# Last-layer products of five sequences among the scans instead of three, and spiking neurons of four on GpSimd instead of three

## The chip, the cores and the metric

The kernel runs on one core of a Trainium2 chip. [...] The metric is device time in microseconds (us) of one launch, stated as the median of several runs.

## What is computed

Eight layers run over 8 sequences of 512 tokens with 128 channels, all in float32. The change touches the end: the state-space mixer of the last but one half layer, its gated feed-forward, and the last layer, a feed-forward whose output goes through a spiking neuron. Cut from the reference, for one sequence `x` (512 x 128):

```python
# mixer: normalise, causal convolution, per-channel step sizes dt, then a scan over time
h[t] = exp(dt[t] * A) * h[t-1] + dt[t] * u[t] * Bmat[t]        # 128 channels x 48 states
y[t] = sum_over_states(h[t] * Cmat[t]);  x = x + y @ out_proj_w.T + out_proj_b
# gated feed-forward
u = rmsnorm(x);  x = x + (silu(u @ gate_w.T) * (u @ up_w.T)) @ down_w.T
# last layer
n = layernorm(x);  c = square(relu(n @ W_fc.T)) @ W_proj.T
mem = 0
for _ in range(5):                      # spiking neuron with a constant input c
    mem = 0.9 * mem + c - reset;  spike = mem > 1;  count += spike
x = x + count / 5
```

The number of spikes in five steps only rises with `c`, so the kernel counts how many of five constants (`SPIKES`) lie below `c`.

## The kernel before

The work that matters is in `l2_attn_l3_attn`. Its last block runs the scans: for each sequence b of 8, four quarters q of the channels, three groups g of 16 states, two halves j. One step of the inner loop makes two pairs of small products into a PSUM tile `bx` (L1879, PE), the decay `a` by an exponential (L1885, ACT), and the scan itself over 128 x 1024 elements (L1890, DVE), 192 scans in all. `give` sums over the states one group later (L1690, PE, tile Z) and multiplies by the gate at a quarter's end (L1698, DVE, tile zx). The inputs of a quarter come from DRAM two quarters ahead (`fetch`, `fetch_dt`, SP's queue), and `products` multiplies the loaded gx by xk on POOL (L1335 in the profile, 128 x 1024 elements) one quarter ahead in the program.

All other work is cut into Python generators, whose steps are placed between the scans. `step(gens)` advances every generator of a list by one yield; `in_turn` chains generators. The list `side` is stepped once behind each group, three times per quarter. It holds:

- `prepare(b)`: normalisation, convolution and step sizes of a later sequence (b + 2 during b). It uses the tiles xn (tag x1, 8 buffers), u, up, xh, dt, du (2 buffers each, up one), and lp and two (one buffer each), the last two for a polynomial on POOL. It is finished for sequence 7 during b = 5.
- `project(b)`: after the last quarter of b: sums over states (L1709), the output projection (L1719, L1720), sums of squares on ACT (L1917), the normalised u (L1732), transposes and copy to hT (L262, L267), two gate products with Silu (L1744, L1746), two up products (L1751, L1752), the down products (L1757), the sum into X[b] with its statistics (L1761, L248, L249). It ends by adding b to `given`.
- `layer_3b(b, tail)`: the last layer up to its output c. It waits (in the program's order) for b in `given`; then normalises (L1122), transposes and copies (L262, L265), makes four products with W_fc (L1795), a Relu and a Square each on ACT (L1803, L1805), then 16 products with W_proj (L1818, each recorded as two), and copies c to a tile y (L1827). With tail False, each of the four products is a step with a PSUM tile of its own and the 16 products are two steps, 8 steps in all; with tail True the four products are two steps and the 16 one, 5 steps, and PSUM comes from the tiles bx and Z of the ended scans.
- `slow_neurons(b)`: the count on POOL: two operations per constant, the sum into X[b] and a store from POOL's own queue (L1849 to L1857). It takes its two work tiles from a gx buffer (tag gx, three buffers, which the scans' loads use).

`neurons(b)` does the count on DVE in five operations and the sum in one (L1835 to L1839), and stores from SP's queue.

PSUM has eight banks: the tag mm (two tiles of one bank) serves prepare, project and layer_3b with tail False; bx takes four banks in two tiles, Z two.

The order is written out by hand by the place of each step: layer_3b of sequences 0 to 2 enters `side` at quarter (5, 3), slow_neurons of 0 to 2 at (7, 2). Behind the last scan, layer_3b of 3 to 7 is stepped with tail True beside what is left in `side`, and neurons(3) to neurons(7) follow as their inputs appear. On each engine the framework may put an instruction ahead of earlier ones in the program that wait for something, as long as tiles and data allow. Layer_3b's normalisation is on POOL for sequences 0 to 4 and on DVE for 5 to 7.

## Time and profile before

| | us |
|---|---|
| median of 3 runs (lowest to highest) | 1713.37 (1712.08 to 1717.24) |
| the profiled execution's own time | 1725.08 |
| its span, first to last instruction | 1723.3 |
| first scan starts | 1129.8 |
| quarter (5, 3) starts its scans | 1495.1 |
| last scan ends | 1654.0 |
| PE's last product ends | 1715.4 |
| DVE's last instruction ends | 1719.8 |
| PE busy over the span | 1470.0 |
| DVE busy over the span | 1206.9 |
| ACT, POOL busy over the span | 796.6, 677.8 |

All times inside an execution are counted from its first instruction. A row of the timeline has the start, the duration of the stretch, the engine, the line, the operation, what it writes and reads, how many instructions were merged and, in brackets, how long the engine had been idle before and what it waited for. A row of a table by windows has a stretch, its length, then the busy time of each engine with the number of its instructions, the granted TensorE clock (1.00 is full), the share of the transfer engines and their GB/s; filtered to one line of the program it has only the engines of that line. PEld are weight loads, which overlap PE's products.

### The profile page before, as it was taken

How to read it: one execution, taken by the hardware profiler on the slowest of the kernel's cores; microseconds unless marked ns; L12 is line 12 of the kernel's file. 1: busy time of each engine (PE TensorE's matmuls, PEld its weight loads, DVE VectorE, ACT ScalarE, POOL GpSimd, SP SyncE). 2: the span in 40 equal slices, each digit the busy share in tenths (PEclk: the TensorE clock that was granted, in tenths of full speed). 3: DMA queues.
4: the chain of work that ended last, by engine and by line, in shares of the span. 5: the costliest groups of instructions: out<-in, count | busy, mean ns of one | idle time of the engine just before them, and what ended most of it. 6: DMA issues, size and time to landing. Idle time of an engine off the chain costs nothing.

```text
span 1723.3 us, 22463 instructions
## 1 busy us (share of the span) xinstructions
PE 1470.0 (85%) x8060; PEld 651.2 (38%) x8061; DVE 1206.9 (70%) x2374; ACT 796.6 (46%) x1158; POOL 677.8 (39%) x728
## 2 busy tenths in 40 slices
PE   5978898899888868988999896977888888888887
PEld 2322333334344435644555453422222222233335
DVE  7688666655654444357775764589899999988765
ACT  3655655555454423353223230055555565565634
POOL 4754344443321140211213318135645645712750
PEclk8999899999899889988999898999899999999988
DMA  7991000000000022304544653634444444443201
GB/s 270 384 342 34 1 1 13 7 13 13 13 19 19 13 99 78 95 10 109 124 116 118 134 126 95 151 80 129 124 127 128 133 129 125 131 117 95 61 13 31
DMA packets 94224, 164.69 MB, mean 96 GB/s; under 512 B 10848, under 2 KB 36960, under 8 KB 90016
## 3 DMA queue, kind: packets, MB, share of 16 engines
q1 hardware_dynamic: 89392, 151.97, 31.4%
q0 software_dynamic: 3568, 9.18, 1.7%
q10 hardware_dynamic: 1152, 2.10, 0.4%
q8 instruction: 64, 1.05, 0.3%
q14 instruction: 48, 0.39, 0.1%
HBM read 110.27 MB, written 52.95 MB: 95 GB/s over the span
## 4 chain that ended last, share of the span: by engine, by line
PE 43%; DVE 28%; issue 10%; POOL 7%; ACT 5%; DMA 5%; SPq 1%; DVEq 0%; POOLq 0%; ACTq 0%
DVE h L1890 11%; PE key L1644 5%; PE acc L1622 5%; PE bx L1879 3%; DMA gx<-du_d 2%; PE mm L262 2%; PE sT L568 2%; DVE mf L547 2%; PE o L591 2%; PE sc L536 1%; PE gu L369 1%; PE gu L1055 1%; DMA gate<-gates 1%; DVE zx L1698 1%; PE Z L1690 1%
## 5 line engine op out<-in xcount | busy, mean ns | idle before, releaser
L1890 DVE TENSOR_TENSOR_SCAN h<-a,bx 128x1024 f32<-128x1024 f32 x192 | 426.9, 2269 | 29.2 <-PE bx L1879 27.7
L1885 ACT ACTIVATE a<-dr,nA 128x1022 f32<-128x1022 f32 x192 | 219.4, 1146 | 221.2 <-DVE h L1890 221.0
L1879 PE MATMUL bx<-gx,wb 64*128 64x512 f32 x768 | 220.2, 666 | 61.3 <-DVE h L1890 59.2
L1335 POOL TENSOR_TENSOR gx<-gx,xk 128x1024 f32<-128x1024 f32 x32 | 75.4, 2357 | 226.0 <-DMA gx<-du_d 194.3
L1644 PE MATMUL key<-xT,L_ffn_keys 128*128 128x512 f32 x256 | 136.4, 615 | 22.9 <-DVE act L1648 22.9
L1879 PEld LDWEIGHTS bx<-gx,wb 64*128 64x128 f32 x768 | 64.8, 195 | 195.1 <-DVE h L1890 149.8
L1622 PE MATMUL acc<-act,L_ffn_values 128*128 128x512 f32 x256 | 132.7, 602 | 0.0
L1648 DVE SCALAR_TENSOR_TENSOR act<-key,gate 128x512 f32<-128x512 f32 x128 | 86.5, 685 | 47.8 <-PE key L1644 34.6
L1690 PE MATMUL Z<-h,wc 64*32 64x512 f32 x1536 | 110.3, 628 | 0.1
L547 DVE TENSOR_REDUCE mf<-sm 128x8 f32<-128x1024 f32 x64 | 76.1, 1211 | 42.5 <-POOL sm L543 42.4
L577 POOL TENSOR_SCALAR_AFFINE_SELECT eT<-eT 128x1024 f32<-128x1024 f32 x64 | 68.9, 1099 | 78.7 <-ACT eT L575 78.7
L543 POOL TENSOR_SCALAR_AFFINE_SELECT sm<-sm 128x1024 f32<-128x1024 f32 x64 | 69.4, 1098 | 71.2 <-ACT sm L542 70.9
L1433 POOL DMA_INDIRECT back<-f_out,back_at x32 | 30.8, 964 | 155.7 <-DVE bn L248 139.3
L542 ACT COPY sm<-sc 128x1024 f32<-128x1024 f32 x64 | 62.5, 1014 | 54.7 <-PE sc L536 40.6
L1410 ACT COPY oT<-acc 128x512 f32<-128x512 f32 x8 | 4.7, 587 | 159.2 <-PE acc L1622 159.2
L575 ACT ACTIVATE eT<-sT 128x1024 f32<-128x1024 f32 x64 | 62.0, 1021 | 28.0 <-PE sT L568 27.9
L1644 PEld LDWEIGHTS key<-xT,L_ffn_keys 128*128 128x128 f32 x256 | 47.1, 195 | 73.2 <-issue 36.2
L1622 PEld LDWEIGHTS acc<-act,L_ffn_values 128*128 128x128 f32 x256 | 49.1, 193 | 60.0 <-issue 60.0
L536 PE MATMUL sc<-kb,qT 32*128 32x512 f32 x256 | 58.9, 724 | 10.0 <-ACT sm L542 4.1
L248 DVE BATCH_NORM_STATS2 bn<-x 128x6 f32<-128x128 f32 x224 | 56.1, 272 | 4.8 <-DMA x<-in_L_attn_hidden_states 4.0
L1116 POOL TENSOR_TENSOR rstd<-rstd,minus_half 128x4 f32<-128x4 f32 x27 | 28.0, 1040 | 80.0 <-DVE rstd L1115 79.8
L568 PE MATMUL sT<-qT,kb 32*128 32x512 f32 x256 | 55.2, 655 | 4.5 <-ACT sm L542 2.9
(482 smaller groups left out, 3006.4 us busy)
## 6 DMA issues: line engine op xcount, KB each, us to landing
f_in<-zeros SPq DMA_DIRECT2D x10, 3584.0 KB
gate<-gates SPq DMA_DIRECT2D x128, 256.0 KB
dr<-dt_d SPq DMA_DIRECT2D x32, 1024.0 KB
gx<-du_d SPq DMA_DIRECT2D x128, 128.0 KB
xk<-xh_d SPq DMA_DIRECT2D x32, 256.0 KB
wide<-in_L_ffn_experts SPq DMA_DIRECT2D x1, 3072.0 KB
xg<-f_in SPq DMA_DIRECT2D x48, 64.0 KB
f_out<-ys SPq DMA_DIRECT2D x12, 256.0 KB
```

The lines of the kernel that those rows point to most:

```text
L536: nc.tensor.matmul(halves[q // 2][:, 4 * (q % 2) : 4 * (q % 2) + 4, :], qT[quad(q), cols(c)], kb[quad(q)], start=True, stop=True,)
L543: nc.gpsimd.affine_select(out=sm, in_=sm, compare_op=ALU.is_ge, fill=-1e30, base=0, pattern=[[0, 8], [-1, P]], channel_multiplier=1,)
L547: nc.vector.tensor_reduce(mf[:, c, 2 * i : 2 * i + 2], sm.rearrange("p (q r) k -> p q r k", q=2), AX.X, ALU.max, negate=True,)
L568: nc.tensor.matmul(halves[q // 2][:, q % 2, :], lhs[quad(q), r, :], rhs[quad(q)], start=(k == 0), stop=(k == 1),)
L1335: nc.gpsimd.tensor_tensor(gx, gx, xk.unsqueeze(1).to_broadcast([P, 2, S]), ALU.mult)
L1622: nc.tensor.matmul(acc, f2_v[:, j, :], act, start=(j == 0), stop=(j == J - 1))
L1644: nc.tensor.matmul(key, f2_k[:, 2 * j : 2 * j + 2, :], xT, start=True, stop=True)
L1648: nc.vector.scalar_tensor_tensor(act, key, 0.0, gate[:, j % 2, :], ALU.max, ALU.mult)
L1690: nc.tensor.matmul(zs[q][32 * j : 32 * j + 32, i, :], wcf[half, g, :], hs[j // 2][half, j % 2, :], start=(g == 0), stop=(g == G - 1),)
L1879: nc.tensor.matmul(bx[:, k, :], wbf[half, g, :], gx[half, j, :], start=True, stop=True,)
L1885: nc.scalar.activation(a[:, :, 1:], dr[:, 2 * j : 2 * j + 2, 1:], AF.Exp, scale=nA[:, q, g : g + 1],)
L1890: nc.vector.tensor_tensor_scan(h.rearrange("p r t -> p (r t)"), a.rearrange("p r t -> p (r t)"), bx.rearrange("p r t -> p (r t)"), 0.0, AL ...
```

## The change

Layer_3b of sequences 0 to 4, not 0 to 2, is made with tail False. Its generators leave `side` for a list of their own, `between`, which enters at the same quarter (5, 3) and is stepped inside the loop over j: behind the first half of every group and behind both halves of the middle one, four times per quarter instead of three. What is left of it behind the last scan runs ahead of layer_3b of 5 to 7. slow_neurons counts for sequences 0 to 3, enters `side` already at (5, 3), and takes its work tiles from the tags lp and two of prepare instead of gx. neurons begins at sequence 4. The engine of the normalisation is now chosen by `tail`.

```diff
-                    normal(b, mv4, r, xn, engine=nc.gpsimd if b < NB - 3 else nc.vector)
+                    normal(b, mv4, r, xn, engine=nc.vector if tail else nc.gpsimd)
...
-                    cnt = work.tile([P, 2, S], F32, tag="gx", name="cnt", bufs=3)
-                    n, hit = cnt[:, 0], cnt[:, 1]
+                    n = work.tile([P, S], F32, tag="lp", name="lp", bufs=1)
+                    hit = work.tile([P, S], F32, tag="two", name="two", bufs=1)
...
-                side = []
+                side, between = [], []
+                TAIL = NB - 3
...
                         if (b, q) == (NB - 3, Q - 1):
-                            side.append(in_turn([layer_3b(k, False) for k in range(3)]))
-                        if (b, q) == (NB - 1, Q - 2):
-                            side.append(in_turn([slow_neurons(k) for k in range(3)]))
+                            between.append(in_turn([layer_3b(k, False) for k in range(TAIL)]))
+                            side.append(in_turn([slow_neurons(k) for k in range(TAIL - 1)]))
...
                                 hs.append(h)
+                                if j == 0 or g == 1:
+                                    step(between)
...
-                side.append(in_turn([layer_3b(b, True) for b in range(3, NB)]))
-                done = 3
+                side.append(in_turn([*between, *(layer_3b(b, True) for b in range(TAIL, NB))]))
+                done = TAIL - 1
```

## The prediction

> **What bounds the kernel now.** I read the page first (TensorE, PE, is busy for 85% of the span, VectorE, DVE, for 70%), then cut the last 600 us into stretches at the starts of the scans (L1890). Sequence 4 lasts from 1382.5 to 1445.8, sequence 6 from 1511.0 to 1582.7, sequence 7 from there to 1654.0, the end of the last scan. The quarter (5, 3), where the last layer's generators enter, begins at 1495.1.

> ```profile
> core 0: us, PE busy (x) PEld busy (x) DVE busy (x) ACT busy (x) POOL busy (x), PEclk, DMA share, GB/s
> ...
> 1382.50:1445.80 63.30, 54.97 (x356) 17.66 (x356) 61.23 (x43) 36.42 (x44) 36.08 (x32) 0.95 0.48 130
> ...
> 1511.00:1582.70 71.70, 63.30 (x408) 24.08 (x410) 61.47 (x43) 43.91 (x57) 16.91 (x12) 0.98 0.39 103
> 1582.70:1654.00 71.30, 61.87 (x404) 22.81 (x400) 61.35 (x41) 34.66 (x46) 51.89 (x40) 0.93 0.23 61
> 1495.10:1654.00 158.90, 137.45 (x884) 50.30 (x868) 137.48 (x94) 84.77 (x108) 78.89 (x62) 0.94 0.33 87
> ...
> 1654.00:1716.00 62.00, 55.56 (x280) 36.51 (x280) 29.64 (x59) 33.80 (x63) 7.63 (x6) 0.92 0.08 22
> ```

> Read the length of each stretch against PE's and DVE's busy time. Sequence 4 is DVE's: 61.2 of 63.3 us. Sequences 6 and 7 hold the same DVE work and take 8 us more: they carry 24 steps of layer_3b for sequences 0 to 2, and PE's work has risen from 55 to 62 or 63 us. Over the nine quarters from 1495.1 the two engines are level (137.45 and 137.48), with 21.4 us in which each is idle. Behind the last scan PE alone sets the pace: 55.6 of 62 us. So there are two prices: what layer_3b's products take from the tail, and what they cost among the scans. The next view, the same two stretches for the two product lines alone (L1795, then L1818), gives both; its first figure behind the length is PE.

> ```profile
> 1495.10:1654.00 158.90, 13.50 (x24) 3.57 (x24) 0.94 0.33 87
> 1654.00:1716.00 62.00, 20.77 (x40) 6.41 (x40) 0.92 0.08 22
> ```
> ```profile
> 1495.10:1654.00 158.90, 12.31 (x96) 11.17 (x96) 0.94 0.33 87
> 1654.00:1716.00 62.00, 23.71 (x160) 22.71 (x160) 0.92 0.08 22
> ```

> Three sequences among the scans: (13.50 + 12.31) / 3 = 8.6 us, and 0.66 for the four transposes (the row at 1539.7), 9.3 us of PE each. Five in the tail: (20.77 + 23.71) / 5 + 0.66 = 9.6 us each.

> **How many steps move.** Before, layer_3b steps once per group, 3 per quarter; 9 quarters make 27 steps, and 3 sequences need 8 each. After, step(between) is called 4 times per quarter (for j = 0 of each group, and j = 1 of the middle one): 36 steps, that is four sequences (32) and four steps of sequence 4: normal, transposes, k = 0 and k = 1. Its other four steps open the tail, ahead of 5, 6 and 7. So 12 steps are added among the scans.

> **Tail.** PE loses sequence 3 (9.6 us) and of sequence 4 the transposes and two of four L1795 products (0.66 + 4.15 / 2 = 2.7): 12.3 us. The copies of y (L1827) in the tail are PE's beat: 1675.1, 1688.4, 1698.0, 1706.3, and PE's end at 1715.4; a sequence is worth 8 to 13 us of it. The chain under it, project(7) to given(7), ends at about 1685 (stats behind L1761 at 1683.0) and then normal, transposes and products of sequence 7, some 12 us at the durations of the rows (four normals 1.1, transposes and copy 1.3, four products with their ACT and DVE work 5, 32 products of L1818 4.7): 1697 even with project(7) as slow as now, against 1715.4 - 12.3 = 1703. So PE still ends last and 12 us is my value. The lower bound is 7: project(7) waits for ACT (the Sqrt and Silu tables, 1.28 us each) with less other work to fill PE, and the rest of sequence 4 now takes the same two mm tiles as project(7), where sequence 3 took bx and Z tiles. The upper is 15, if the half clock behind such waits (granted 0.65 from 1671 to 1674 and 0.60 from 1710 to 1713) goes. neurons(3), 3.9 us of DVE (0.43 + 4 x 0.69 + 0.69), also leaves the tail, at no gain: DVE is busy there for 30 of 62 us.

> **Scans.** PE gains 9.3 + 0.66 + 13.50 / 6 = 12.2 us, to 149.6, and becomes the busier engine. How much of it lengthens the 158.9 us depends on the idle 21.4. 14.7 us of that are bx products waiting for a scan (15 waits), which is free room; 6.4 us are three stalls in which PE waits for ACT. Bounds: if all idle time stays, +12.2; if quarters become as tight as the one from 1511.0 to 1526.7 (PE 15.52 of 15.7 us) and 1582.7 to 1597.6 (14.54 of 14.9), some 0.3 to 1.0 us idle each, 149.6 + 9 = 158.6, no change. Another price: 158.9 less nine quarters of sequence 4's 63.3 / 4 is 16.5 us for 24 steps, 0.69 each, 8.3 for 12. I take **+5**: a little below the middle of 0 and 12.2, because waits for scans are two thirds of the idle time and a busier PE has no such waits.

> **GpSimd (POOL).** A sequence of slow_neurons takes 17.3 us (first is_gt at 1627.67, store issued until 1644.94). Before, three run back to back from 1610.3 to 1662.3. After, four, each behind its own y, some 31 us apart (8 steps at 4 per quarter of 15.5 us), so POOL goes from 78.9 us to 78.9 + 17.3 + 7.6 (what now lies behind 1654) = 104 of about 164. What queues behind them is products (L1335, 2.36 us per quarter), project's two steps (1.04 each) and the normals (3.1). POOL waits 68.6 us for the gx loads there, and products for the last quarter ran at 1605.9 for scans from 1639.4: 20 us and more of slack against 17.3. Cost nothing; without that cover, one slow step (2.8 us) per quarter. The 13 scans from 1612 on, with POOL busy all through, take 2255 to 2287 ns like those before (2253 to 2289), so DVE is not slowed. The tiles lp and two were last used by prepare(7) (du at 1496.4), and slow_neurons fills them in order on one engine: no wait for a buffer. The normals of 3 and 4 already run on POOL among the scans (1554.5, 1595.6); the edit of `engine` chooses the same engines as before. ACT gets 6.1 us for sequence 3 (two copies 0.59, four pairs of 0.58 + 0.63) and 3.1 for 4, on 84.8 of 158.9: not a bound in sum, but its order matters below. The stores move from SP to POOL's queue for one sequence, 0.84 us.

> **Sum**: -12 + 5 = **-7 us**, against the profiled execution's own 1725.08 (span 1723.3 and 1.8 around it): 1718.1. That execution is 11.7 us above the median of the runs, 1713.37; the same 7 us off the median give 1706.4.

> **Rivals.**
> *Slower: stalls for the two mm tiles.* The place is the third quarter of a sequence, 25.0 us in sequence 6 and 26.8 in 7 where others take 15. Timeline:

> ```profile
> 1617.14 1.15 ACT L1885 ACTIVATE a<-dr,nA 128x1022 f32<-128x1022 f32 x1 [1.03 <-DVE h L1890]
> 1618.20 0.58 ACT L1803 ACTIVATE du<-mm 128x512 f32<-128x512 f32 x1
> ...
> 1618.83 2.08 PE L1744 MATMUL mm<-hT,L_attn_gate_w 128*128 128x512 f32 x2 [2.53 <-ACT du L1803]
> ...
> 1620.83 3.78 PE L1879 MATMUL bx<-gx,wb 64*128 64x512 f32 x8
> ...
> 1623.03 2.29 DVE L1890 TENSOR_TENSOR_SCAN h<-a,bx 128x1024 f32<-128x1024 f32 x1 [4.80 <-PE bx L1879]
> ```

> project's second gate product needs an mm tile that layer_3b's product filled; ACT empties it only after an exponential that waits for a scan; PE stands for 2.53 us with the next bx products behind, restarts at a granted clock of 0.50 (next row), and DVE loses 4.80 us.

> ```profile
> 1618.80:1621.00 2.20, 2.17 (x4) 0.67 (x5) 0.00 (x0) 2.16 (x3) 2.03 (x3) 0.50 0.00 0
> ```

> Twelve more steps through two tiles can make more of these. 12 / 4.80 = 2.5 further stalls eat the tail's gain; with four the sum is -12 + 19.2 = +7.2, 1720.6. For it: in each of the two sequences the stall came where both generators met. Against: the new calls stand at j = 0, with an exponential and a scan between them and project's step. [...]

> *No change*: PE's 12.2 us come back in full among the scans, -12 + 12.2: 1713.4. For it: PE would be the busiest engine there. Or the tail gives only 7: 1711.

> *Larger gain*: steps apart from project's remove half of the 10 us by which each third quarter is too long: 2 x 5 = 10 less in the scans against PE's +5, tail -12: -17, 1696.4. For it: a relu of layer_3b then has its turn on ACT ahead of the exponential that held it at 1617.14. Against: both still share ACT and two tiles.

> **Chances.** Forecast 0.45, larger gain 0.17, no change 0.20, slower 0.18. A measurement of this kernel tells about 0.3%, 5.1 us, from no change. Of the forecast, 0.35 lies beyond that and 0.10 within; with 0.17 and 0.02 of the others faster is 0.54, same 0.26, slower 0.20. The range runs from 1696 (-12 - 5) to 1719 (three to four stalls); what it leaves out is the worse half of the slower case and the end of the large gain, below 2 in 10.

> **What would show it.** The last scan ends at 1654 + 5, PE busy near 150 us from quarter (5, 3) to there; third quarters near 25 us; four copies of y ahead of the last scan in place of three; PE busy 43 us behind it, PE's end 50 us behind it in place of 61.4. POOL has no product later than its bx needs it. Wrong: bx waits for POOL, third quarters of 30 us, or a tail still above 58 us because project(7) waits.

## The result, and the profile after

The changed kernel takes 1738.21 us (median of 4 runs, 1735.43 to 1742.1) against 1715.3 (median of 4, 1712.08 to 1718.5) for the kernel before: a ratio of 1.0135 (95% interval 1.0105 to 1.0165), 23 us slower, where 7 us faster was forecast. The profiled execution took 1735.43 us, span 1733.7.

First two lines of the page: the engines' busy time (PE is TensorE, DVE VectorE, ACT ScalarE, POOL GpSimd), and the scans with the idle time ahead of them; the third line is that of the scans in the page of before.

```profile
PE 1473.9 (85%) x8060; PEld 647.6 (37%) x8061; DVE 1203.9 (69%) x2368; ACT 795.5 (46%) x1158; POOL 691.5 (40%) x740
L1890 DVE TENSOR_TENSOR_SCAN h<-a,bx 128x1024 f32<-128x1024 f32 x192 | 427.4, 2268 | 44.9 <-PE bx L1879 44.8
```
```profile
L1890 DVE TENSOR_TENSOR_SCAN h<-a,bx 128x1024 f32<-128x1024 f32 x192 | 426.9, 2269 | 29.2 <-PE bx L1879 27.7
```

Busy times are those of before within 4 us on PE, DVE and ACT: the engines have no more work. What grew is DVE's idle time ahead of the scans, from 29.2 to 44.9 us over the whole span, and what ends it is bx, PE's product; from quarter (5, 3) on alone, DVE's waits for bx go from 11.7 to 36.8 us. So PE delivers late, and the question is what PE waits for. The stretches tell where: the quarters (6, 0), (6, 1) and (6, 2), then all nine quarters from (5, 3) to the end of the last scan, then the tail; below them (6, 1) of the kernel before.

```profile
1506.30:1527.50 21.20, 18.21 (x133) 8.21 (x134) 15.12 (x10) 10.84 (x13) 4.53 (x3) 1.00 0.44 118
1527.50:1551.10 23.60, 14.19 (x85) 4.23 (x82) 14.39 (x9) 11.47 (x21) 22.91 (x20) 0.87 0.37 103
1551.10:1578.20 27.10, 24.76 (x136) 10.63 (x136) 17.85 (x17) 13.13 (x15) 5.70 (x4) 0.99 0.25 67
1491.30:1681.30 190.00, 150.67 (x936) 55.95 (x920) 141.15 (x97) 92.64 (x123) 102.71 (x80) 0.96 0.27 75
1681.30:1726.00 44.70, 39.98 (x228) 26.65 (x228) 22.67 (x49) 25.47 (x48) 0.00 (x0) 1.00 0.08 22
```
```profile
1526.70:1541.90 15.20, 13.79 (x108) 6.20 (x104) 14.45 (x10) 9.06 (x17) 5.67 (x4) 1.00 0.37 103
```

The second line is unlike its counterpart of before: in 23.6 us PE works 14.2, DVE 14.4, and the fifth pair, POOL, 22.91 in place of 5.67. An engine that the prediction put aside is the only busy one. The last two lines of the first block hold the balance. The scans from (5, 3) take 190.0 us instead of 158.8, +31; from the last scan to the end of the span it takes 52.4 instead of 69.4, -17. That is +14 by the two profiles.

Lengths of the quarters in us, each from its first scan to the next quarter's, here and for all kernels that were run. They are those of one profiled execution each; the ratio is that of several runs.

| kernel | (5,3) | (6,0) | (6,1) | (6,2) | (6,3) | (7,0) | (7,1) | (7,2) | (7,3) | scans | tail | ratio to before (95%) |
|---|---|---|---|---|---|---|---|---|---|---|---|---|
| before | 15.8 | 15.7 | 15.2 | 25.0 | 15.8 | 14.8 | 15.1 | 26.8 | 14.5 | 158.8 | 69.4 | 1 |
| before, again | 14.7 | 15.8 | 16.2 | 26.6 | 15.6 | 14.8 | 15.1 | 25.3 | 14.3 | 158.4 | 67.7 | one run |
| after | 15.0 | 21.2 | 23.6 | 27.2 | 16.8 | 21.2 | 23.6 | 27.2 | 14.3 | 190.0 | 52.4 | 1.0135 (1.0105 to 1.0165) |
| after, again | 15.1 | 21.2 | 23.6 | 27.2 | 16.8 | 21.2 | 23.6 | 27.2 | 14.3 | 190.1 | 52.4 | one run |
| products only | 14.5 | 22.7 | 14.4 | 26.9 | 15.4 | 22.7 | 15.3 | 27.6 | 14.3 | 173.8 | 53.2 | 1.0035 (1.0011 to 1.0059) |
| neurons only | 15.3 | 15.8 | 15.2 | 24.6 | 15.8 | 14.8 | 24.6 | 23.7 | 14.3 | 164.1 | 66.3 | 1.0054 (1.0038 to 1.0070) |
| shorter count | 14.6 | 21.2 | 14.4 | 26.9 | 18.0 | 22.7 | 18.5 | 26.9 | 14.3 | 177.4 | 52.9 | 1.0022 (1.0001 to 1.0044) |
| u off POOL | 16.3 | 21.6 | 15.1 | 27.5 | 15.6 | 23.2 | 16.2 | 27.5 | 14.3 | 177.3 | 52.3 | 1.0036 (1.0010 to 1.0062) |
| step apart | 16.1 | 18.4 | 18.7 | 24.5 | 14.7 | 18.4 | 21.1 | 23.6 | 14.3 | 169.9 | 52.4 | 0.9982 (0.9955 to 1.0009) |
| products only, step apart | 14.7 | 18.4 | 15.1 | 23.6 | 14.7 | 18.4 | 17.1 | 23.6 | 14.3 | 159.9 | 55.7 | 0.9957 (0.9940 to 0.9974) |
| products only, step first | 15.0 | 18.9 | 14.3 | 24.3 | 15.3 | 18.9 | 18.9 | 24.4 | 14.3 | 164.3 | 56.4 | 0.9978 (0.9956 to 0.9999) |
| step apart, u off POOL | 14.9 | 18.6 | 15.9 | 23.6 | 14.8 | 18.6 | 17.6 | 23.6 | 14.3 | 161.8 | 52.3 | 0.9947 (0.9923 to 0.9970) |
| products only, Square on POOL | 15.0 | 27.1 | 14.4 | 30.2 | 15.1 | 28.3 | 15.3 | 52.7 | 14.3 | 212.5 | 52.3 | 1.0252 (1.0207 to 1.0297) |
| products only, Square on DVE | 15.1 | 20.0 | 14.4 | 24.9 | 15.0 | 20.0 | 16.0 | 25.4 | 14.3 | 165.1 | 55.8 | 1.0000 (0.9973 to 1.0027) |

The table shows two losses: the second quarters, (6, 1) and (7, 1), go from 15 to 23.6 us, and the first ones, (6, 0) and (7, 0), from 15 to 21.2.

**Loss 1, quarters (6, 1) and (7, 1).** The timeline of the changed kernel for (6, 1), POOL's, PE's and DVE's rows:

```profile
1525.28 1.51 POOL L1849 TENSOR_SCALAR lp<-x 128x512 f32<-128x512 f32 x1 [7.03 <-ACT x L1827]
...
1541.28 1.27 POOL L1856 TENSOR_TENSOR x<-x,lp 128x512 f32<-128x512 f32 x1
1542.50 2.35 POOL L1335 TENSOR_TENSOR gx<-gx,xk 128x1024 f32<-128x1024 f32 x1
1544.80 1.05 POOL L1727 TENSOR_TENSOR r<-r,minus_half 128x4 f32<-128x4 f32 x1
1545.80 0.87 POOL L1857 DMA_DIRECT2D out<-x  x1
1546.68 1.06 POOL L1732 TENSOR_TENSOR u<-x,r 128x512 f32<-128x512 f32 x1
...
1547.80 1.11 PE L262 MATMUL mm<-ident,u 128*128 128x128 f32 x4 [7.74 <-POOL u L1732]
1548.85 2.08 PE L1879 MATMUL bx<-gx,wb 64*128 64x512 f32 x4
...
1551.07 2.29 DVE L1890 TENSOR_TENSOR_SCAN h<-a,bx 128x1024 f32<-128x1024 f32 x1 [9.21 <-PE bx L1879]
```

Read from the bottom. DVE loses 9.21 us for a bx product; PE could not make it, because project(5)'s transposes stood ahead of it in PE's queue and waited 7.74 us for u. On POOL u waits for r, and both stand behind the whole count of sequence 0 (1525.28 to 1542.5) and behind one more product, L1335. The sum that DVE prepares for r (L1726) was done at 1529.8. How much room u had without the count is seen in "products only" (below). Its quarter (6, 1) starts at 1524.81:

```profile
1530.84 1.04 POOL L1732 TENSOR_TENSOR u<-x,r 128x512 f32<-128x512 f32 x1
...
1537.32 0.66 PE L262 MATMUL mm<-ident,u 128*128 128x128 f32 x4
```

There u is ready 7.1 us after the start of the quarter and PE comes to the transposes at 12.5: 5.4 us of room. In the changed kernel, where the quarter starts at 1527.48, PE comes as early, at 12.6 (1540.06), but u is ready only at 20.3: 13.2 us later, 7.7 more than the room. The same happens in (7, 1), with 6.0 us of room and 13.1 of delay: PE waits 6.53 us, DVE 7.64. In the kernel before, where r and u stand behind a product L1335 that waits for its load, the room was smaller still: u was ready at 1538.49 and PE came at 1539.72, and in its second profile PE waited 1.25 us for u in (6, 1).

The placing of rows in a queue is the framework's: the count now stands where y of sequence 0 arrives, ahead of the steps that wait for later things. Before, it entered at (7, 2) with tiles from gx and ran from 1610 on, behind all of this. Whether the early entry or the free tiles lp and two moved it, no run separates.

**Loss 2, quarters (6, 0) and (7, 0).** ACT's, PE's and DVE's rows in (6, 0):

```profile
1511.84 0.58 ACT L1803 ACTIVATE du<-mm 128x512 f32<-128x512 f32 x1
...
1514.09 1.15 ACT L1885 ACTIVATE a<-dr,nA 128x1022 f32<-128x1022 f32 x1 [1.68 <-DVE h L1890]
1515.15 0.61 ACT L1805 ACTIVATE du<-du 128x512 f32<-128x512 f32 x1
1515.81 0.49 PE L1818 MATMUL mm<-L_ffn_W_proj,du 128*128 128x128 f32 x2 [2.98 <-ACT du L1805]
...
1521.24 2.29 DVE L1890 TENSOR_TENSOR_SCAN h<-a,bx 128x1024 f32<-128x1024 f32 x1 [5.01 <-PE bx L1879]
```

The extra step in the middle group puts the last (k = 3) of layer_3b's four products with W_fc and the first half of its L1818 products one scan apart. Between them ACT has to make a Relu and a Square, and the Square (L1805) stands in ACT's queue behind an exponential that itself waits for a scan: the Relu ends at 1512.42, the Square starts at 1515.15. PE waits 2.98 us and DVE 5.01; in (7, 0) 2.63 and 5.01. Together the four stalls cost DVE 26.9 us, against +31 for the scans. Not all of the 5.01 is the Square's: between it and bx PE also works off 4.2 us of products (1515.81 to 1520.00).

### The profile page after: what moved, and what is told of

Same layout as the page of the kernel before. It is cut to its first block, busy times and chain, and to the rows that moved or that the text cites. A ratio compares the mean times of both kernels' runs of the same rounds, so it can differ in the third digit from the quotient of the medians.

```text
span 1733.7 us, 22473 instructions
## 1 busy us (share of the span) xinstructions
PE 1473.9 (85%) x8060; PEld 647.6 (37%) x8061; DVE 1203.9 (69%) x2368; ACT 795.5 (46%) x1158; POOL 691.5 (40%) x740
## 4 chain that ended last, share of the span: by engine, by line
PE 44%; DVE 28%; issue 9%; POOL 9%; ACT 6%; DMA 3%; SPq 1%; DVEq 0%; POOLq 0%; ACTq 0%
DVE h L1890 11%; PE key L1644 4%; PE acc L1622 4%; PE bx L1879 4%; PE mm L262 2%; PE sT L568 2%; PE Z L1690 2%; DMA gate<-gates 2%; PE o L591 2%; PE mm L1250 2%; DVE mf L547 2%; PE sc L536 2%; PE gu L369 2%; PE gu L1055 1%; DVE zx L1698 1%
## 5 line engine op out<-in xcount | busy, mean ns | idle before, releaser
L1890 DVE TENSOR_TENSOR_SCAN h<-a,bx 128x1024 f32<-128x1024 f32 x192 | 427.4, 2268 | 44.9 <-PE bx L1879 44.8
L1885 ACT ACTIVATE a<-dr,nA 128x1022 f32<-128x1022 f32 x192 | 219.4, 1146 | 221.2 <-DVE h L1890 221.0
L1879 PE MATMUL bx<-gx,wb 64*128 64x512 f32 x768 | 219.7, 659 | 59.6 <-DVE h L1890 55.8
L1335 POOL TENSOR_TENSOR gx<-gx,xk 128x1024 f32<-128x1024 f32 x32 | 75.4, 2356 | 170.3 <-DMA gx<-du_d 147.8
L1879 PEld LDWEIGHTS bx<-gx,wb 64*128 64x128 f32 x768 | 62.9, 191 | 193.5 <-DVE h L1890 146.0
L1690 PE MATMUL Z<-h,wc 64*32 64x512 f32 x1536 | 112.2, 627 | 1.0 <-DVE h L1890 1.0
L547 DVE TENSOR_REDUCE mf<-sm 128x8 f32<-128x1024 f32 x64 | 76.1, 1211 | 44.5 <-POOL sm L543 44.5
```

What stands on the lines that cost most here:

```text
L547: nc.vector.tensor_reduce(mf[:, c, 2 * i : 2 * i + 2], sm.rearrange("p (q r) k -> p q r k", q=2), AX.X, ALU.max, negate=True,)
L1335: nc.gpsimd.tensor_tensor(gx, gx, xk.unsqueeze(1).to_broadcast([P, 2, S]), ALU.mult)
L1690: nc.tensor.matmul(zs[q][32 * j : 32 * j + 32, i, :], wcf[half, g, :], hs[j // 2][half, j % 2, :], start=(g == 0), stop=(g == G - 1),)
L1879: nc.tensor.matmul(bx[:, k, :], wbf[half, g, :], gx[half, j, :], start=True, stop=True,)
L1885: nc.scalar.activation(a[:, :, 1:], dr[:, 2 * j : 2 * j + 2, 1:], AF.Exp, scale=nA[:, q, g : g + 1],)
L1890: nc.vector.tensor_tensor_scan(h.rearrange("p r t -> p (r t)"), a.rearrange("p r t -> p (r t)"), bx.rearrange("p r t -> p (r t)"), 0.0, AL ...
```

## The experiments

Theory P: POOL's order (loss 1) and theory A: ACT's order behind the doubled step (loss 2), each on its own and each curable alone. The rival to both is the price per step: twelve more steps cost PE what they cost, wherever they stand. It turns out to hold in part, in the first quarters (see "products only, step apart"). A second rival is the prediction's own, stalls for the two mm tiles in the third quarters.

**Products only.** layer_3b as changed; the count as before, for three sequences.

```diff
-  n = work.tile([P, S], F32, tag="lp", name="lp", bufs=1)
-  hit = work.tile([P, S], F32, tag="two", name="two", bufs=1)
+  cnt = work.tile([P, 2, S], F32, tag="gx", name="cnt", bufs=3)
+  n, hit = cnt[:, 0], cnt[:, 1]
-  side.append(in_turn([slow_neurons(k) for k in range(TAIL - 1)]))     # at (NB-3, Q-1)
+  side.append(in_turn([slow_neurons(k) for k in range(3)]))            # at (NB-1, Q-2)
-  done = TAIL - 1
+  done = 3
```

> The products' half of the change alone: five sequences in small steps, but slow_neurons as before (sequences 0 to 2, from quarter (7, 2), in gx buffers). Theory P, GpSimd's order: in the changed kernel project's u (L1732) stands behind a whole count of slow_neurons, PE waits for it 7.7 and 6.5 us and DVE 9.2 and 7.6; here u has POOL to itself, so quarters (6, 1) and (7, 1) fall from 23.5 to about 15.5 us and the time by about 16.9, 1738 - 17 = 1721. Quarters (6, 0) and (7, 0) stay at 21.2. Rival L, PE's load (12 more steps on the busiest engine cost what they cost, wherever POOL works): the scans still take 185 to 190 us from (5, 3) on and the time stays at 1733 to 1740.

Measured: 1723.8 us, ratio 1.0035. (6, 1) and (7, 1) are back at 14.4 and 15.3 us, no wait for u is left, and the scans lose 16.2 of the 31 us, about the 16.85 that DVE lost at the two waits. (6, 0) and (7, 0) do not fall, they take 22.7: loss 2 belongs to the products alone. The 1.5 us above the 21.2 of the changed kernel go with the granted clock, 0.92 over the quarter against 1.00 (last section).

**Neurons only.** The kernel before, with the count of its three sequences in lp and two and entering at (5, 3).

```diff
-  cnt = work.tile([P, 2, S], F32, tag="gx", name="cnt", bufs=3)
-  n, hit = cnt[:, 0], cnt[:, 1]
+  n = work.tile([P, S], F32, tag="lp", name="lp", bufs=1)
+  hit = work.tile([P, S], F32, tag="two", name="two", bufs=1)
-  if (b, q) == (NB - 1, Q - 2):                                        # slow_neurons enters
+  if (b, q) == (NB - 3, Q - 1):
```

> The neurons' half alone: the kernel before, with slow_neurons of sequences 0 to 2 from quarter (5, 3) on in the tiles lp and two. Theory P says that the harm needs both halves: with the old steps y of sequence 0 comes at about 1539, behind u of project(5) (1537.5), and the count of sequence 1 ends at about 1606, ahead of u of project(6) (1609): same as before within 3 us, 1712 to 1718. A theory by which early counts on POOL are bad by themselves: 1725 to 1735. Rival L: same as before, as PE's work is.

Measured: 1725.29 us, ratio 1.0054. One project met a count: in (7, 1) PE waits 7.86 us for u, and that quarter is 24.6 us instead of 15.1. In (6, 1) there is none, since with three steps a quarter y of sequence 0 comes only at 1531.56, and u had gone through POOL at 1530.34. Where I had expected no change of this kernel I missed that the count of the next sequence reaches POOL ahead of project(6) all the same. So the move of the neurons costs some 9 us even without one more product among the scans.

**Shorter count.** The changed kernel, with three of the five constants left out of the count on POOL.

```diff
-  for th in SPIKES[1:]:
+  for th in SPIKES[1:2]:
```

> The changed kernel, but slow_neurons compares with two of the five constants instead of all (it leaves out part of the count for sequences 0 to 3), so a count holds POOL for about 9 us in place of 17.3; PE's, ACT's and DVE's work and every place of a step are as in the changed kernel. Theory P: u of project(5) and project(6) is no longer late, quarters (6, 1) and (7, 1) fall to 15 to 17 us, the time by 14 to 17: 1721 to 1724. Rival L: 1736 to 1740 as the changed kernel.

Measured: 1722.74 us, ratio 1.0022. It leaves out three pairs of 2.9 us, 8.7 us of each count, more than PE's wait of 7.74; no wait for u is left and (6, 1) is 14.4 us. The length of the count is the cause, not the tiles it uses. (The edit also takes three steps of `side` from each count; "u off POOL", next, leaves them.) (6, 3) and (7, 1) stay at 18 us; in (7, 1) PE waits 2.54 us for a scan, and why is open.

**u off POOL.** The changed kernel; project(5) and project(6) make r on ACT and DVE (inv_sqrt), and u on DVE, as project(7) always did.

```diff
-  if b < NB - 1:                                   # r by POOL's power
+  if b < NB - 3:
-  engine = nc.gpsimd if b < NB - 1 else nc.vector  # u, and the sum into X
+  engine = nc.gpsimd if b < NB - 3 else nc.vector
```

> The changed kernel with project's root, u and sum of X for sequences 5 and 6 moved off POOL, as they are for 7 already (Sqrt on ACT, the rest on DVE); slow_neurons keep their place, buffers and work. Theory P: nothing of project queues behind a count, quarters (6, 1) and (7, 1) fall from 23.6 to 16 or 17 us (with 1.4 us more of DVE and two table loads of 1.28 us on ACT each), the time by 13 to 16: 1722 to 1725. A theory by which the counts disturb through something else (SBUF, the loads' products, the y copies): 1733 to 1740.

Measured: 1723.3 us, ratio 1.0036. Four full counts stay on POOL where they were, and only what queued behind them is moved; (6, 1) is 15.1 us. Rows of its timeline:

```profile
1526.26 0.69 DVE L1732 TENSOR_TENSOR u<-x,rstd 128x512 f32<-128x512 f32 x1
...
1534.26 1.28 POOL L1856 TENSOR_TENSOR x<-x,lp 128x512 f32<-128x512 f32 x1
```

u is ready 8 us before the count ends. With the shorter count and this one theory P is shown from both ends, by what stands in front and by what stands behind.

**Step apart.** The changed kernel; the doubled step goes from the middle group to the last.

```diff
-  if j == 0 or g == 1:
+  if j == 0 or g == 2:
```

> The changed kernel with one condition altered: the doubled step of a quarter stands in the last group, not the middle one. Theory A (L1818 waits for the Square of k = 3, which stands behind a waiting exponential): quarters (6, 0) and (7, 0) fall from 21.2 to about 18.4 and the third quarters from 27.2 to 23.6, as from the products' half (22.7, 26.9) to that with the step apart, 13 us together. Theory P: u of project stays among the operations of a count in POOL's order (behind seven or eight of them and a waiting product in place of nine and a product), so quarters (6, 1) and (7, 1) stay 4 to 9 us too long. Together 1715 to 1726. If the two are not additive but one stall in two guises, it would come down to 1709.

Measured: 1715.07 us, ratio 0.9982. The first quarters fall from 21.2 to 18.4 us and the third from 27.2 to 24.5 and 23.6; (6, 1) and (7, 1) also shrink, to 18.7 and 21.1, as y and so the count start at another time, but remain 3.6 and 4.0 us longer than without the early count (15.1 and 17.1 in the next run); PE waits for u there 1.86 us in (6, 1) and not at all in (7, 1), where the rest is not explained. In all the scans lose 20.1 us.

**Products only, step apart.** Both edits: those of "products only" and `g == 2`.

> As e1_products_only, and the doubled step of a quarter moved from the middle group to the last one, so that a whole group lies between layer_3b's fourth product (k = 3) and its first half of L1818. Theory A, ACT's order: in quarters (6, 0) and (7, 0) L1818 waits 2.6 to 3.0 us for the Square of k = 3, which stands behind an exponential that waits for a scan; DVE loses 5.0 us and the quarter 5.5 to 6.3. Here these quarters fall from 21.2 to about 15.7, the time by 11 to 12 against e1_products_only: 1709 to 1711 if P holds too, that is faster than before by some 5 us. Rival L: no better than e1_products_only, the idle time moves elsewhere.

Measured: 1709.39 us, ratio 0.9957, faster than before. The scans take 159.9 us with twelve more steps among them, against 158.8: +1.1. But the first quarters are 18.4 us, not the 15.7 that I expected. The row of (6, 0):

```profile
1501.60:1520.00 18.40, 18.40 (x134) 8.24 (x135) 15.21 (x8) 11.84 (x17) 2.36 (x1) 1.00 0.47 129
```

PE is busy throughout; before, it was 15.5 us in the same quarter. So the wait for the Square was 2.8 of the 5.5 to 6.4 us by which the first quarters had grown, and 2.7 to 3.6 us each are the load of the added steps, the rival's price. The third quarters, which fall below those of before (23.6 against 25.0 and 26.8), give most of it back.

**Step apart, u off POOL.** The edits of "u off POOL" and `g == 2`: all four counts on POOL, all five products among the scans, as the change wants it.

> Both edits in the changed kernel: the step apart and project's u of sequences 5 and 6 off POOL. If the two stalls are all that the change cost, it keeps the tail of the change (52 to 55 us in place of 69) and comes to 1708 to 1713, ahead of the kernel before. If PE's load had a price of its own: 1716 to 1725.

Measured: 1707.28 us, ratio 0.9947, the fastest of all. Its window of the nine quarters:

```profile
1491.40:1653.20 161.80, 140.51 (x936) 53.35 (x920) 142.55 (x102) 97.56 (x129) 95.80 (x74) 1.00 0.32 87
```

The same 936 products as in the changed kernel, in 161.8 us instead of 190.0, at a clock of 1.00; over all nine DVE is the busier engine, in (6, 0) and (7, 0) PE. The tail is the same to 0.1 us. What the change meant to do works, once neither queue blocks.

**Products only, step first.** `g == 0` in place of `g == 1`, so that the doubled step stands in the first group.

> As e1_products_only, the doubled step in the first group. Then k = 3 comes at the second half of group 0 and the first half of L1818 at the first half of group 1: as near as in e1_products_only, one half later, but with give's products and project's step between. Theory A as a matter of distance in scans: quarters (6, 0) and (7, 0) near 20 to 22.7, 1720 to 1724. If it is rather a matter of which group carries two steps beside project's step: 16 to 18.5, 1708 to 1713.

Measured: 1710.38 us, ratio 0.9978. By the distance in halves alone it should have been as slow as the middle group; it was not: (6, 0) and (7, 0) are 18.9 us. In the first group PE has the products of give (L1690) between the k = 3 product and L1818, those of project only behind it, and waits 0.93 us for the Square instead of 2.98. So the number of halves alone does not decide; what PE still has to do in between counts as well.

**Products only, Square on POOL.** A direct test of theory A: the Square of k = 3 leaves ACT's queue.

```diff
+  if not tail and k == 3:
+      nc.gpsimd.tensor_tensor(t, t, t, ALU.mult)
-  if b < NB - 1:
+  elif b < NB - 1:
       nc.scalar.activation(t, t, AF.Square)
```

> The kernel with layer_3b's change alone, and the Square of its k = 3 product taken off ACT: GpSimd multiplies du by itself there (its queue is nearly empty in those quarters). If ACT's order is the cause of the long quarters (6, 0) and (7, 0), because the Square stands behind an exponential that waits for a scan, PE's wait ahead of L1818 falls from 3.0 to some 1.1 us (the multiplication's 1.3 us in place of 0.6 behind the exponential's), the two quarters from 22.7 to 20 or 21, and the time from 1723.8 to about 1719. If the distance between steps matters for another reason, the quarters stay above 22 and the time at 1722 to 1726. If the multiplication itself comes late on GpSimd, PE waits there for L1804 on GpSimd instead.

Measured: 1760.96 us, ratio 1.0252, the slowest of all: my expectation that POOL's queue was nearly empty there failed. It is empty of work but not free. POOL's rows in (6, 0), then PE's in (7, 2):

```profile
1518.84 2.35 POOL L1335 TENSOR_TENSOR gx<-gx,xk 128x1024 f32<-128x1024 f32 x1 [12.88 <-DMA gx<-du_d]
1521.15 1.04 POOL L1805 TENSOR_TENSOR du<-du 128x512 f32<-128x512 f32 x1
```
```profile
1674.95 0.80 PE L1820 MATMUL mm<-L_ffn_W_proj,du 128*128 128x128 f32 x2 [25.13 <-POOL du L1805]
```

The multiplication needs 1.04 us, but ahead of it the product of a gx that is still being loaded blocks the queue for 12.88 us; PE waits 6.92 us (11 for DVE). In (7, 2) it lands behind the counts and PE waits 25.13. For theory A the run decides nothing; for the general form of theory P it is the strongest case.

**Products only, Square on DVE.** The same test on a queue with room: the product stands between two scans of a group.

```diff
-  if b < NB - 1:
+  if b < NB - 1 and (tail or k < 3):
       nc.scalar.activation(t, t, AF.Square)
   else:
       nc.vector.tensor_tensor(t, t, t, ALU.mult)
```

> Again the kernel with layer_3b's change alone, with the Square of the k = 3 product among the scans on DVE instead of ACT; there it stands between the scans of the two halves of a group, so it waits for no exponential and is done 0.69 us behind the first of the two scans. The run on GpSimd could not tell, since that queue was blocked. If the place in ACT's queue makes the long quarters (6, 0) and (7, 0), PE's wait ahead of L1818 falls from 3.0 to some 2.0 us, the granted clock is not halved behind it, the two quarters come from 22.7 to 19 or 20, and the time from 1723.8 to 1716 to 1720, less than with the doubled step moved to the last group (1709.4), which also shortens the third quarters. If the queue is not the cause, DVE only has 0.69 us more four times: quarters of 22.7 to 23.4, time 1723 to 1727.

Measured: 1716.92 us, ratio 1.0000, within the expected 1716 to 1720. Rows of (6, 0):

```profile
1511.69 0.66 DVE L1807 TENSOR_TENSOR du<-du 128x512 f32<-128x512 f32 x1
1511.81 1.15 ACT L1886 ACTIVATE a<-dr,nA 128x1022 f32<-128x1022 f32 x1 [1.68 <-DVE h L1891]
...
1512.41 0.49 PE L1818 MATMUL mm<-L_ffn_W_proj,du 128*128 128x128 f32 x2 [1.87 <-DVE du L1807]
```

The Square no longer waits for the exponential, only for the scan ahead of it on DVE; PE's wait falls from 2.98 to 1.87 us and the quarter from 22.7 to 20.0, of which some 1.5 us go with the granted clock, by an estimate from the 21.2 us of the changed kernel, where the wait of 2.98 left it at 1.00; behind the wait it is 1.00 here and was 0.50 in "products only". Theory A holds for the wait: the Square's place in a queue makes it. It does not hold for the whole growth of the first quarters: 18.4 us ("step apart") is what they take without any wait of PE, 2.7 to 3.6 more than before.

**Before, again, and after, again.** The two kernels unedited, one more profile each.

> The kernel before once more, for a second profile of it; nothing is edited. If the first profiled execution (1725.08 us, scans from (5, 3) 158.8, behind the last scan 69.4) was a long one by chance, this one has scans plus tail of 222 to 225 us in place of 228.2, its tail near the 66.3 that the kernel with the neurons alone showed, and an own time near 1715. If it shows 228 again, the difference between stages and medians has another cause.

> The changed kernel once more, unedited. Its waits should come again at the same places: PE for u of project(5) and project(6) on GpSimd some 7 us each, for the Square some 3 us each, scans from (5, 3) of 188 to 192 us, tail of 52 to 53. If the places or prices change from execution to execution, the split of the loss into two causes is weaker than the single profile made it look.

Measured: 1720.13 us (scans plus tail 226.1) and 1736.59 (242.5). The changed kernel repeats quarter by quarter to 0.1 us: its two losses are fixed by the order of the queues. Of before I had expected 222 to 225; the second profile explains 2 us and no more. By stages the change costs 14 to 16 us, by medians 23. Both profiles of before, 1725.08 and 1720.13, lie above the medians of its runs (1715.3 to 1719.09, from one set of runs to the next), and for the ten edited kernels the two ways of reckoning differ by up to some 6 us as well ("products only" is 1 us longer than the second profile of before by stages and 7 by medians). The start of (5, 3), ahead of every edit, varies from 1483.7 to 1499.9 us over the profiles of this study. So the remaining 7 us are near what this comparison can tell; where they lie stays open.

## Why the prediction was wrong

- **The step that failed** is the paragraph on GpSimd: "Cost nothing; without that cover, one slow step (2.8 us) per quarter." It listed what queues behind a count, "products (L1335, 2.36 us per quarter), project's two steps (1.04 each) and the normals (3.1)", and then took the slack of the first, 20 us against 17.3, for all of them. project's u had 5.4 and 6.0 us ("products only"), and 1.2 and 0.5 in the kernel before (ready at 1538.49 and 1610.31, asked for at 1539.72 and 1610.84). The price was two waits that cost DVE 16.85 us, and without them (products only) 16.2 us of the scans were gone. The mark chosen for POOL, "no product later than its bx needs it", came true and said nothing, since the wrong instruction was watched; none of the three signs named under "Wrong" appeared either.
- **It was to be seen in the profile of before**, 280 us ahead of the change. The rows where project of the first sequence meets a POOL that waits for a load:

```profile
1216.49 2.35 POOL L1335 TENSOR_TENSOR gx<-gx,xk 128x1024 f32<-128x1024 f32 x1 [8.20 <-DMA gx<-du_d]
1218.80 1.02 POOL L1727 TENSOR_TENSOR r<-r,minus_half 128x4 f32<-128x4 f32 x1
1219.89 1.04 POOL L1732 TENSOR_TENSOR u<-x,r 128x512 f32<-128x512 f32 x1
...
1220.99 1.11 PE L262 MATMUL mm<-ident,u 128*128 128x128 f32 x4 [4.94 <-POOL u L1732]
```

  The chain POOL, r, u, transposes, bx, scan is there whole, with PE losing 4.94 us and the next scan 5.50. The prediction uses no row from there.
- **Scans, "+5".** With both queues mended the scans grow by 1.1 us (three counts on POOL) to 3.0 us (four) net, so the price per step was not too low. It is a sum of two: the first quarters are 2.7 to 3.8 us longer each, and the third ones 1.4 to 3.2 shorter. The upper bound of +12.2 took PE's busy time for a fixed amount of work, and it isn't: the same 936 products are 150.67 us busy in the changed kernel at a mean clock of 0.96, and 140.51 at 1.00. That 150.67 agrees with the forecast 149.6 is chance. What the bounds left out was a third kind of idle time, new waits.
- **"The new calls stand at j = 0, with an exponential and a scan between them and project's step"** was the argument against stalls. One of the four calls stands at j = 1, and the argument looked at project only. Layer_3b's own chain, product, Relu, Square, next product, has the exponential in its middle, and the doubled step left it no time: 2.98 and 2.63 us of PE, 10 us of DVE in the first quarters. The third ones are 3.6 us shorter with the step apart (23.6 against 27.2), and some 2 us shorter with the Square alone moved (24.9 and 25.4 against 26.9 and 27.6).
- **The slower rival** had the right pattern, PE standing still at one product with the next bx behind it, and the wrong wait, place and price. Its count of four agrees by luck: two stalls wait for u from POOL and two for a Square, none for an mm tile. The third quarters, where it was placed, grew by 0.4 to 2.2 us each; the four stalls lie in the first and second quarters and cost 26.9 us, not 4 x 4.80 = 19.2.
- **Tail, "-12".** It fell by 17.0 (15.3 against the second profile of before), above the upper bound of 15. PE is busy 39.98 us behind the last scan against the forecast 43, at a clock of 1.00 against 0.92: the half clock behind the waits went as well, which the bound of 15 had named. PE's end lies 44.5 us behind the last scan, not 50.
- **"Larger gain"** said that steps apart from project's shorten the third quarters. They do, by 2 us each against before, when the doubled step stands in the last group; in the change as made they were longer.

With both queues mended and all else as the change has it (step apart, u off POOL) the stages give +3 - 17 = -14 against the first profile of before, and the medians 1707.28 - 1717.55 = -10.3. The forecast's two terms were too cautious, by 2 to 4 and by 5 us; what it left out, the new waits, was worth most of the 28 us between the changed kernel and this one (242.4 against 214.1 us for scans and tail); the third quarters, 3.6 us shorter each, hold the rest.

## What to carry to other kernels

Before work is put on an engine "with room", list every instruction that comes to stand behind it in that engine's order, and for each one the time from when it is done now to when its reader asks for it; the smallest of these is the room (5.4 us here, 1.2 in the kernel before), not the engine's idle share and not the slack of the commonest one. An idle engine may be blocked by an instruction that waits for a load, as POOL was for 12.88 us. Where a small step feeds a later step through another engine, give PE other products between the two, and look for existing waits of the same chain anywhere in the trace, not only near the edit.

## What the runs showed of the hardware

The same wait had two outcomes for the clock. Behind 2.98 us of idle PE the changed kernel ran on at 1.00 in (6, 0); in "products only", behind an equal 2.98, the granted clock fell to 0.50, and DVE lost 6.57 us instead of 5.01. Behind 7.74 us it was 0.50 until the next scan, behind 1.87 it was 1.00.

```profile
1509.13:1512.54 3.41, 0.96 (x8) 0.96 (x9) 2.87 (x2) 2.17 (x3) 1.99 (x1) 1.00 0.52 136
1512.54:1515.96 3.42, 3.42 (x28) 0.88 (x31) 0.00 (x0) 0.65 (x1) 0.37 (x1) 0.50 0.52 115
```
```profile
1510.62:1514.03 3.41, 2.21 (x11) 1.04 (x10) 3.41 (x4) 1.63 (x2) 0.00 (x0) 1.00 0.39 135
1514.03:1517.44 3.41, 1.63 (x18) 1.37 (x26) 2.21 (x2) 2.81 (x3) 1.56 (x1) 1.00 0.53 124
```

The wait of "products only" lies for 2.45 us in one stretch (PE busy 0.96 of 3.41), and the next stretch runs at half the clock. That of the changed kernel is split, 1.20 us idle in one stretch and 1.78 in the next, and the clock stays. In the traces of before and after, cut into such stretches from 1200 us on, the clock fell behind each of the 16 full-clock stretches with more than 1.9 us of idle PE, behind none of the 252 with less than 1.4, and behind four of the 11 in between. So in these traces the length of one wait does not tell the two outcomes apart, 2.98 us stand on both sides, and the idle time of the stretch does where it is outside of 1.4 to 1.9 us. What sets the clock no run shows.
